# A two-layer GRU run in chunks: 32 steps and 16 times 62 in place of 16 times 64

## The chip, the cores and the metric

The kernel runs on one NeuronCore of a Trainium2 chip. The metric is the device time of one execution in microseconds (us). Engines are named as the profile names them: PE is the matrix engine (PEld its weight load), DVE the vector engine, ACT the scalar engine, POOL the GpSimd engine, SP the engine that issues most DMAs. "L324" is line 324 of the kernel before.

## What is computed

The input is x, two sequences (b) of 1024 tokens of 256 numbers, and a context vector for each sequence. A residual block with a two-layer GRU comes first, then a residual mixture of experts over all 2048 tokens. Cut to what matters here:

```
mixed = tanh(x @ W_in.T + b_in + context)
for layer in (0, 1):                        # h starts at zero for each sequence
    xr, xz, xn = split(x_t @ Wih.T + bih)   # x_t: mixed, or layer 0's h
    hr, hz, hn = split(h @ Whh.T + bhh)
    r, z = sigmoid(xr + hr), sigmoid(xz + hz)
    n = tanh(xn + r * hn)
    h = (1 - z) * n + z * h                 # 1024 steps, each needs the one before
x = x + (gate * h2 + h2) @ W_out.T + b_out  # gate: of the context
x = x + (shared(x) + two best of 8 experts(x)) / 3
```

All arithmetic that matters is in float32.

## The kernel before, in words

**Chunks.** The 1024 steps of a sequence are cut into J = 16 chunks of S = 64 steps. With B = 2 sequences that makes R = 32 rows, and one step of a layer does all 32 rows at once. A chunk's true start state is the end of the chunk before it, which is not known yet. So layer 0 goes through its chunks twice: a first pass of `AHEAD[0]` = 64 steps from zero, whose end states, moved on by one row, are the start states of the second pass, which gives the outputs. The row of each sequence that holds its first chunk starts the second pass from zero. Layer 1 starts its first pass 44 steps ahead (`AHEAD[1]`) and runs `LAG` = 2 ticks behind layer 0. After the second pass `fit` (L441) compares the end state of each row with the start state that the next row was given. If any of the 128 partitions is off by more than 2^-18 of the largest start value (`TOL`), a branch at L678 does all 1024 steps one after the other and repeats the rest.

**Layout.** Tokens are kept in the order (step in chunk, b, chunk), 32 columns to a step: a *group*. `x_sb` holds x, `hs1` layer 1's outputs, `inputs` the 64 groups of layer 0's input sums, all on chip. A state lies in two forms: units on partitions, `h` (128 x 2 x 32), for the matrix engine, and a *row* form (128 x 64, four quarters of the units times 32 rows) for the gates. One 32x32-block transpose on DVE (L332) goes from the second to the first.

**A step of a layer.** `add_state` (L262): 8 matmuls of the state with `Whh` into a PSUM bank that ACT has filled with the input sums (`prepare`, L460 to L466). `finish_scanned` (L296): ACT sigmoid (L305), DVE scan (L308), ACT tanh (L319), DVE L321, DVE scan (L324), DVE transpose (L332). Layer 1's input products are fed by `feed` (L468).

**Ticks.** The loop at L594 is written out: tick t does layer 0's step and, while layer 1 runs, layer 1's. `position` (L453) tells the step in the pass: 0 is the first of the second pass. In the kernel before, layer 0 is alone in ticks 0 to 21, both layers run in ticks 22 to 127, and layer 1 is alone in 128 and 129: 130 ticks, 128 + 108 = 236 layer steps.

**Work placed between the steps.** The input side is made in pieces while the loop runs: 16 *mix* pieces (L207: 4 matmuls and two tanh for half of 8 groups) and 64 *input* pieces (L386: 8 matmuls, and a DVE add at L396 for one group). `work_of` (L503) gives a tick of layer 0 alone three units of pieces (a mix counts two), and a tick of both layers one piece. The order is fixed by `pieces_in_turn` (L522), and the pieces must be there before the step that reads them. In the second pass `plan` (L557) places, for each 8 finished groups, the output projection (L805), the adding to x (L816), the transposing back to tokens (L821, L843), the router (L832) and the store of the tokens to DRAM (L877). The order on each engine in this loop is the order of the program text.

**Pass change.** At position 0 `begin_from` (L437) clears one column for the two first chunks and hands on the state tile moved by one column, and `turned` (L432) makes its row form. Both stand at the top of the tick. Behind the loop come the last group of 8, the fit, and the mixture of experts (`moe`, L899), which the change leaves as it is.

Of the kernel before, what the change touches and what calls it, by code (L numbers as in the profile page):

```python
# [17 lines left out]
P = 128  # L18
# [12 lines left out]
J = R // B  # L31
S = T // J


AHEAD = (64, 44)

# [23 lines left out]
EARLY = 8  # L60
FILL = EARLY + 1


# [8 lines left out]
def gru_moe(ctx, tc, xT, vec, bias, w_in, wih0, whh0, wih1, whh1, w_out, w_gate, router, w1, w3, w2, w1e, w2e, out):  # L72
# [29 lines left out]

    inputs = const.tile([P, S, 4, U], FP, name="inputs")
    room = inputs.rearrange("p s c u -> p s (c u)")
# [9 lines left out]
    for k in range(KD):  # L114
        nc.vector.tensor_scalar(
            mix_bias[:, k, :],
            vec_sb[:, COND + k * B : COND + (k + 1) * B],
            vec_sb[:, B_IN + k : B_IN + k + 1],
            None,
            ALU.add,  # L120
        )

    class Steps:
# [171 lines left out]

        def finish_scanned(self, layer, to, tick, before_n, after_n, between):  # L296

# [33 lines left out]
            )  # L331
            nc.vector.transpose(to, row[:, :, 1])  # L332
            self.rows[layer], self.states[layer] = row[:, :, 1], to

# [25 lines left out]
    with ExitStack() as stack:  # L360
# [23 lines left out]
        spread(0)  # L384

        def input_piece(i):  # L386

            ps = g.bank("ps_in")[:, 0 : 3 * U].rearrange("p (c u) -> p c u", c=3)

            def products():  # L390
                at = i * R % MB
                mixed = mixes[i * R // MB]
                return g.times_input(0, ps, lambda k: mixed[:, k, at : at + R], True)

            def rest():
                nc.vector.tensor_tensor(inputs[:, i, 1:4, :], ps, g.sum_bias[0][:, 1:4, :], ALU.add)  # L396

            return products, rest, lambda: None
# [18 lines left out]

        ahead = [edge.tile([P, KD, 1 + R], FP, name=f"ahead{layer}") for layer in range(2)]  # L420
        for t in ahead:
            nc.gpsimd.memset(t, 0.0)

        def given(layer, name, end):

            t = edge.tile([P, KD, R], FP, name=f"{name}{layer}")
            nc.gpsimd.memset(t, 0.0)
            for b in range(B):
                nc.vector.tensor_copy(t[:, :, b * J + 1 : (b + 1) * J], end[:, :, b * J : (b + 1) * J - 1])
            return t  # L430

# [4 lines left out]

        def begin_from(layer):  # L437
            nc.vector.memset(ahead[layer][:, :, J : J + 1], 0.0)
            return ahead[layer][:, :, 0:R]

        def fit(layer):  # L441

            off = edge.tile([P, KD, R], FP, name=f"off{layer}")
            nc.vector.tensor_tensor(off, given(layer, "end", g.states[layer]), g.starts[layer], ALU.subtract)
            off = turned(off.rearrange("p k r -> p (k r)"), f"off_row{layer}")
            most = edge.tile([P, 2], FP, name=f"most{layer}")
# [6 lines left out]
        def position(layer, tick):  # L453

            return tick - AHEAD[0] - LAG * layer

        def runs(layer, tick):
            return -AHEAD[layer] <= position(layer, tick) < S

        def prepare(layer, tick):  # L460

            if runs(layer, tick):
                return nc.scalar.copy(  # L463
                    by_sum(banks[layer][tick % 2])[:, 0:4, :],
                    g.sum_bias[1] if layer else inputs[:, position(0, tick) % S, :, :],
                )  # L466

        def feed(tick, halves):  # L468

            if halves and runs(1, tick):  # L470
                fed = h0[tick - LAG]
                return g.times_input(
                    1, by_sum(banks[1][tick % 2])[:, 1:4, :], lambda k: fed[:, k, :], False, True, halves
                )

        def let_wait(ins, copied):
# [17 lines left out]
        def input_pieces():  # L494
            for i in range(S):
                yield input_piece(i)
# [25 lines left out]
        def pieces_in_turn():  # L522

            for _ in range(MB // R, S, MB // R):
                for which in (mixing, making, mixing, *[making] * (MB // R - 1)):
# [31 lines left out]
        def plan(group):  # L557
            first = AHEAD[0] + LAG + (group + 1) * GS
            for i, (m, b) in enumerate((m, b) for m in range(KD) for b in range(B)):
# [11 lines left out]

        for group in range(S // GS - 1):
            plan(group)
# [15 lines left out]
        g.negate(nc.gpsimd, g.wih[1], 1)  # L589
        g.negate(nc.gpsimd, g.whh[1], 2)  # L590


        with tc.manual_schedule():
            for tick in range(AHEAD[0] + S + LAG):  # L594
                now = [layer for layer in range(2) if runs(layer, tick)]
                for layer in now:
                    if layer not in g.states:
                        g.states[layer], g.rows[layer] = zero_state, zero_row
                    elif position(layer, tick) == 0:
                        g.starts[layer] = g.states[layer] = begin_from(layer)  # L600
                        g.start_rows[layer] = g.rows[layer] = turned(g.starts[layer], f"start_row{layer}")
# [3 lines left out]
                for layer in now:  # L605
# [3 lines left out]
                    if layer == 0:  # L609
                        last = placed(tick, "product")  # L610
                        last = do(work, 0) or last
                        if not busy:
                            feed(tick + 1, [0])
                        to = h0_pool.tile([P, KD, R], FP, name="h0")
                        if position(0, tick) == -1:
                            to = ahead[0][:, :, 1:]
                        h0[tick] = to
                        g.finish_scanned(
# [4 lines left out]
                            lambda: copied.append(prepare(0, tick + 1)),  # L623
                            lambda: (do(work if 1 in now else [], 1), placed(tick, "scan0")),
                        )
                    else:
                        last = feed(tick + 1, range(KD) if busy or 0 not in now else [1])
                        if 0 not in now:
                            placed(tick, "product")
                        to = hs1[:, :, cols(position(1, tick) % S)]  # L630
                        if position(1, tick) == -1:
                            to = ahead[1][:, :, 1:]
                        g.finish_scanned(
# [4 lines left out]
                            lambda: prepare(1, tick + LAG),  # L638
                            lambda: (0 in now or placed(tick, "scan0"), placed(tick, "scan1")),
                        )  # L640
                if 1 not in now:
                    do(work, 1)
# [21 lines left out]

            front.all_of(g.bank, S // GS - 1, rest_of_hidden)
            assert not places
# [11 lines left out]
    with tc.If(n_fit < P):  # L678
        with ExitStack() as stack:

            g = Steps(stack, "_turn", on_pe=True, rest_of_x=lambda: load_x(0, N))
            all_mixed = room[:, 0 : KD * N // D, :].rearrange("p (k s) d -> p k (s d)", k=KD)
            for n0 in range(0, N, MB):
# [8 lines left out]
            for t in (*turn_rows, *turn_states, column):  # L692
                nc.vector.memset(t, 0.0)
            with tc.For_i(0, T, 1) as t:
                chunk = t >> (S.bit_length() - 1)
                chunk.max_val = J - 1
                n = (t & (S - 1)) * R + chunk
                for b in range(B):
# [8 lines left out]
                for b in range(B):  # L707
                    for k in range(KD):
                        nc.vector.tensor_copy(hs1[:, k, bass.ds(n + b * J, 1)], turn_states[1][:, k, b : b + 1])
            for group in range(S // GS):  # L710
                front.all_of(g.bank, group)
# [5 lines left out]
class Front:  # L717
# [133 lines left out]
    def hid(self, m, n):  # L851

        more = self.room[:, NT + ROWS : S, :].rearrange("p (m s) d -> p m (s d)", m=KS - KD)
        return self.h1[:, m, n] if m < KD else more[:, m - KD, n]
# [453 lines left out]
```

## Time and profile before

| what | us |
|---|---|
| median of the runs shown (three: 553.87, 554.26, 555.28) | 554.26 |
| the profiled execution, its own time | 558.67 |
| its span, from first to last instruction | 556.9 |
| first L324 of the loop (tick 0) | 12.81 |
| last L324 of the loop (tick 129) | 379.12 |
| PE busy / DVE busy / ACT busy / POOL busy | 521.6 / 393.5 / 249.6 / 76.8 |

The profiled execution is 4.4 us above the median, and its span is 1.8 us shorter than its own time. Lengths of ticks are read as the distance between starts of layer 0's L324 in one tick and in the next. The loop takes 366.3 of the 556.9 us; some 13 us of loading lie ahead of it, and the rest behind it is the mixture of experts. The granted clock of the matrix engine was 0.995 over the span.

### The profile page before, as it was taken

Reading aid. Unit: us, or ns where it says so; the run is one execution under the profiler, and the core shown is the slowest. Engines: PE = TensorE matmul, PEld = TensorE weight load, DVE = VectorE, ACT = ScalarE, POOL = GpSimd, SP = SyncE. Lnnn points to the kernel's source line nnn. Section 1 sums busy time; section 2 is a strip of 40 time slices with the busy share of each in tenths; the row PEclk is TensorE's granted clock in tenths of the full one; section 3 lists DMA queues with packets and bytes.
Section 4 is the critical chain, followed back from the end, with each engine's and each line's share of the span. In section 5 each row is a group of like instructions: output and inputs, shape, how many; then the busy total and the mean of one; then the engine's idle time right before and its main releaser. Section 6 shows DMA issues by size and latency. Waiting matters only on the chain.

```text
span 556.9 us, 18850 instructions
## 1 busy us (share of the span) xinstructions
PE 521.6 (94%) x7620; PEld 345.1 (62%) x7620; DVE 393.5 (71%) x1309; ACT 249.6 (45%) x850; POOL 76.8 (14%) x131
## 2 busy tenths in 40 slices
PE   6999999999999899999989999989998999999994
PEld 3666666666555445666656656655447888864683
DVE  3776679889888788888888888897972333322395
ACT  3433356666666555556565565652122333341000
POOL 1200000000000000000000000001054444007771
PEclk9999999999999999999999999999998999999999
DMA  8970000000000000000000000002023433213253
GB/s 282 366 237 1 2 3 4 3 2 4 3 3 3 2 2 2 2 22 2 22 23 1 22 22 4 22 1 77 1 67 104 124 124 122 68 58 105 87 166 106
DMA packets 22785, 31.62 MB, mean 57 GB/s; under 512 B 3009, under 2 KB 18241, under 8 KB 22689
## 3 DMA queue, kind: packets, MB, share of 16 engines
q1 hardware_dynamic: 19328, 21.52, 11.4%
q0 software_dynamic: 3216, 8.79, 5.5%
q8 instruction: 64, 1.05, 0.8%
q14 instruction: 33, 0.26, 0.2%
q10 hardware_dynamic: 144, 0.01, 0.0%
HBM read 21.00 MB, written 9.31 MB: 54 GB/s over the span
## 4 chain that ended last, share of the span: by engine, by line
DVE 41%; PE 35%; ACT 9%; issue 6%; POOL 4%; DMA 3%; another core or an unknown queue 1%; SPq 0%; DVEq 0%; POOLq 0%; ACTq 0%
DVE row L324 14%; DVE ps_step L308 13%; DVE h L332 8%; ACT n L319 8%; PE ps_step L265 7%; PE ps_in L237 6%; PE ps_y L1134 6%; PE ps_h L1134 5%; POOL inputs L1211 3%; PE ps_w L859 3%; PE ps_mix L214 3%; DMA x_sb<-in_xT 2%; PE ps_hT L1126 1%; PE ps_step L237 1%; PE ps_xT L1126 1%
## 5 line engine op out<-in xcount | busy, mean ns | idle before, releaser
L265 PE MATMUL ps_step<-whh_sb,h 128*32 128x192 f32 x3712 | 198.0, 331 | 6.2 <-DVE h L332 5.2
L265 PEld LDWEIGHTS ps_step<-whh_sb,h 128*32 128x32 f32 x3712 | 98.1, 109 | 73.3 <-DVE h L332 53.0
L324 DVE TENSOR_TENSOR_SCAN row<-gates,n 128x128 f32<-128x128 f32 x236 | 100.3, 425 | 33.4 <-ACT n L319 33.0
L308 DVE TENSOR_TENSOR_SCAN ps_step<-gates,ps_step 128x128 f32<-128x128 f32 x236 | 99.4, 421 | 20.4 <-ACT gates L305 20.0
L237 PE MATMUL ps_step<-wih_sb,h 128*32 128x192 f32 x1712 | 106.2, 328 | 5.1 <-ACT ps_step L463 1.5
L319 ACT ACTIVATE n<-ps_step 128x64 f32<-128x64 f32 x236 | 55.0, 233 | 114.7 <-DVE ps_step L308 114.7
L305 ACT ACTIVATE gates<-ps_step 128x128 f32<-128x128 f32 x236 | 68.4, 290 | 41.7 <-PE ps_step L265 36.0
L237 PEld LDWEIGHTS ps_step<-wih_sb,h 128*32 128x32 f32 x1712 | 58.1, 109 | 33.7 <-ACT ps_step L463 20.9
L332 DVE STREAM_TRANSPOSE h<-row 128x64 f32<-128x64 f32 x234 | 57.5, 246 | 8.0
L859 PE MATMUL ps_w<-x_sb,w_sb 128*128 128x512 f32 x128 | 56.7, 596 | 0.1
L237 PE MATMUL ps_in<-wih_sb,mixed 128*32 128x192 f32 x1024 | 51.4, 327 | 2.6 <-DVE wih_sb L172 2.6
L463 ACT COPY ps_step<-inputs 128x256 f32<-128x256 f32 x128 | 49.6, 388 | 3.6 <-DVE inputs L396 3.6
L1128 DVE COPY hT<-ps_hT 128x256 f32<-128x256 f32 x35 | 14.9, 425 | 51.0 <-PE ps_hT L1126 47.5
L926 POOL IOTA lane_i<- 128x128 int32 x1 | 0.2, 240 | 366.4 <-PE ps_fit L671 366.4
L321 DVE SCALAR_TENSOR_TENSOR n<-gates,row 128x64 f32<-128x64 f32 x232 | 48.6, 209 | 0.0
L237 PEld LDWEIGHTS ps_in<-wih_sb,mixed 128*32 128x32 f32 x1024 | 33.6, 110 | 13.8 <-issue 5.0
L463 ACT COPY ps_step<-bt 128x256 f32<-128x256 f32 x108 | 40.6, 376 | 3.4
L859 PEld LDWEIGHTS ps_w<-x_sb,w_sb 128*128 128x128 f32 x128 | 23.9, 190 | 28.0 <-issue 26.3
L1163 POOL DMA_INDIRECT inputs<-given,pick x35 | 33.4, 954 | 52.6 <-PE ps_xT L1126 26.5
L1134 PE MATMUL ps_y<-w2e_sb,hT 128*128 x140 | 37.2, 389 | 3.3 <-DVE hT L1128 3.3
L1134 PE MATMUL ps_h<-w1e_sb,xT 128*128 x140 | 36.4, 383 | 0.7 <-DVE h L873 0.7
L1211 POOL DMA_INDIRECT inputs<-back,slots x32 | 31.1, 973 | 35.5 <-DMA back<-y 26.4
(168 smaller groups left out, 451.3 us busy)
## 6 DMA issues: line engine op xcount, KB each, us to landing
back<-y SPq DMA_DIRECT2D x35, 128.0 KB
w1e_sb<-in_w1e SPq DMA_DIRECT2D x1, 2048.0 KB
w2e_sb<-in_w2e SPq DMA_DIRECT2D x1, 2048.0 KB
given<-inputs SPq DMA_DIRECT2D x8, 256.0 KB
out_dram<-o SPq DMA_DIRECT2D x16, 128.0 KB
wih_sb<-in_wih SPq DMA_DIRECT2D x2, 768.0 KB
whh_sb<-in_whh SPq DMA_DIRECT2D x2, 768.0 KB
x_sb<-in_xT SPq DMA_DIRECT2D x3, 512.0 KB
```

What stands on the lines that cost most here:

```text
L237: last = nc.tensor.matmul(out=out[cols(q), :, :], lhsT=given(k), rhs=self.wih[layer][:, k, q * 3 * U : (q + 1) * 3 * U].rearrange("p (g u) ...
L265: nc.tensor.matmul(out=by_sum(self.sums[layer])[cols(q), 0:3, :], lhsT=self.states[layer][:, k, :], rhs=self.whh[layer][:, k, q * 3 * U : ...
L305: nc.scalar.activation(gates[:, :, :, 1], sums[:, 1:3, :], AF.Sigmoid)
L308: nc.vector.tensor_tensor_scan(s, gates[:, 0, :, :].rearrange("p u i -> p (u i)"), ps[:, 0 : 6 * U : 3], 0.0, ALU.mult, ALU.add,)
L319: nc.scalar.activation(n[:, :, 0], s[:, 1 : 2 * U : 2], AF.Tanh, scale=-1.0)
L321: nc.vector.scalar_tensor_tensor(n[:, :, 1], gates[:, 1, :, 1], 1.0, h, ALU.subtract, ALU.mult)
L324: nc.vector.tensor_tensor_scan(row.rearrange("p u i -> p (u i)"), gates[:, 1, :, :].rearrange("p u i -> p (u i)"), n.rearrange("p u i -> p ...
L332: nc.vector.transpose(to, row[:, :, 1])
L463: return nc.scalar.copy(by_sum(banks[layer][tick % 2])[:, 0:4, :], g.sum_bias[1] if layer else inputs[:, position(0, tick) % S, :, :],)
L859: last = self.tc.nc.tensor.matmul(out=ps, lhsT=self.later[name][:, k, m * P : (m + 1) * P], rhs=self.x1[:, k, blk * TB : (blk + 1) * TB], ...
L1134: nc.tensor.matmul(out=ps, lhsT=of[:, k, :], rhs=weights_sb[:, bass.ds(e * KD + k, 1), :], start=(k == 0), stop=(k == KD - 1),)
L1211: nc.gpsimd.indirect_dma_start(out=yb, out_offset=None, in_=back[:, :], in_offset=bass.IndirectOffsetOnAxis(ap=slots[:, i % 2, i // 2 : i ...
```

## The change

Each sequence is now 32 steps and 16 chunks of 62 (32 + 16 * 62 = 1024). In the first pass row 0 of each sequence does 30 steps whose results are thrown away; then its state is set to zero (`kept`), and in the last 32 steps of the pass it does the first 32 tokens, as final outputs, not as a trial run. In the second pass row j (1 to 15) does chunk j - 1, starting from what row j - 1 ended the first pass with, and row 0 does the last chunk, starting from row 15's end. Row 1's start is exact, so its column is taken out of the fit. Ticks: layer 0 alone in 0 to 19, both in 20 to 123, layer 1 alone in 124 and 125: 126 ticks, 124 + 106 = 230 layer steps. Layer 1's first pass stays 44 steps.

The output still has 64 groups. The two extra ones (`EXTRA` = 2) stand in front and hold the first 32 tokens of each sequence; the passes use groups 2 to 63. Row 0 thus has other inputs in the first pass (the first 32 tokens) than in the second (the last chunk), and three things move data for it: `exchange` swaps 32 columns of x for each sequence (six copies on POOL), `last_inputs` writes row 0's input sums for the second pass from groups 0 and 1 to DRAM and back to groups 32 to 63 (three DMAs from SP), and `first_outputs` copies row 0's outputs of the first pass into groups 0 and 1 (two copies on POOL). Two POOL memsets for `ahead` and two for `end` go.

The diff, cut to its core (the branch for a failed fit, whose sequential loop becomes two loops, and renamings of 64 to `GROUPS` are left out; the lines at the end, of layer 0, stand likewise for layer 1):

```diff
-S = T // J
-AHEAD = (64, 44)
+FIRST = 32
+S = (T - FIRST) // J
+AHEAD = (S, 44)
+GROUPS = N // R
+EXTRA = FIRST // J
...
+    def exchange():
+        other = const.tile([P, KD, B, FIRST], FP, name="other")
+        for to, of in ((other, None), (None, x_sb), (x_sb, other)):
+            for e in range(EXTRA):
...
+                nc.gpsimd.tensor_copy(a, b)
...
         def finish_scanned(self, layer, to, tick, before_n, after_n, between, keep=None):
...
-            nc.vector.transpose(to, row[:, :, 1])
-            self.rows[layer], self.states[layer] = row[:, :, 1], to
+            row = row[:, :, 1]
+            if keep is not None:
+                kept = self.edge.tile([P, U], FP, name=f"kept{layer}")
+                nc.vector.tensor_scalar(kept, row, keep, None, ALU.mult)
+                row = kept
+            nc.vector.transpose(to, row)
+            self.rows[layer], self.states[layer] = row, to
...
+        not_first = g.gru_only.tile([P, 1], FP, name="not_first")
+        row_i = g.gru_only.tile([P, 1], I32, name="row_i")
+        nc.gpsimd.iota(row_i, pattern=[[0, 1]], base=0, channel_multiplier=1)
+        nc.vector.tensor_scalar(row_i, row_i, J - 1, None, ALU.bitwise_and)
+        nc.vector.tensor_copy(not_first, row_i)
+        nc.vector.tensor_scalar(not_first, not_first, 1.0, None, ALU.min)
...
-        def begin_from(layer):
-            nc.vector.memset(ahead[layer][:, :, J : J + 1], 0.0)
-            return ahead[layer][:, :, 0:R]
+        def go_round(layer):
+            to, of = by_row(begin[layer]), by_row(g.states[layer])
+            nc.vector.tensor_copy(to[:, :, :, 1:J], of[:, :, :, 0 : J - 1])
+            nc.vector.tensor_copy(to[:, :, :, 0:1], of[:, :, :, J - 1 : J])
...
         def fit(layer):
...
-            nc.vector.tensor_tensor(off, given(layer, "end", g.states[layer]), g.starts[layer], ALU.subtract)
+            nc.vector.tensor_tensor(off[:, :, :, 1:J], end[:, :, :, 0 : J - 1], begun[:, :, :, 1:J], ALU.subtract)
+            nc.vector.tensor_tensor(off[:, :, :, 0:1], end[:, :, :, J - 1 : J], begun[:, :, :, 0:1], ALU.subtract)
+            nc.vector.memset(off[:, :, :, 1:2], 0.0)
...
+        def keep_of(layer, tick):
+            return not_first[:, 0:1] if position(layer, tick) == -FIRST - 1 else None
...
-            for i in range(S):
+            for i in (*range(EXTRA, MB // R), *range(EXTRA), *range(MB // R, GROUPS)):
                 yield input_piece(i)
...
         def plan(group):
-            first = AHEAD[0] + LAG + (group + 1) * GS
+            first = AHEAD[0] + LAG + (group + 1) * GS - EXTRA
...
+        def last_inputs():
+            nc.sync.dma_start(
+                out=spare.rearrange("e p d -> p e d"), in_=inputs[:, 0:EXTRA, :, :].rearrange("p e c u -> p e (c u)")
+            )
+            for e in range(EXTRA):
+                at = GROUPS - FIRST + e * J
+                nc.sync.dma_start(
+                    out=room[0:P:J, at : at + J, :], in_=spare[e, :, :].rearrange("(r i) d -> r i d", i=J)
+                )
+        def first_outputs():
+            for e in range(EXTRA):
...
+                nc.gpsimd.tensor_copy(by_row(hs1[:, :, cols(e)]), row)
+        place(AHEAD[0] - 1, "end", exchange)
+        place(AHEAD[0], "end", last_inputs)
+        place(AHEAD[0] + LAG, "end", first_outputs)
...
-                        g.starts[layer] = g.states[layer] = begin_from(layer)
+                        g.starts[layer] = g.states[layer] = begin[layer]
                         g.start_rows[layer] = g.rows[layer] = turned(g.starts[layer], f"start_row{layer}")
...
-                        if position(0, tick) == -1:
-                            to = ahead[0][:, :, 1:]
...
+                            keep_of(0, tick),
                         )
+                        if position(0, tick) == -1:
+                            go_round(0)
```

`go_round` stands right behind the layer's own step, ahead of the other layer's; `begin_from` stood at the top of the next tick. In the changed program's order of instructions `exchange`'s first two copies stand ahead of POOL's two negations of layer 1's weights (L172), and its other four behind them.

## The prediction, made before the changed kernel ran

> **What bounds the kernel now.** I read the page's busy times first, then its chain by lines, then the timeline tick by tick.
>
> ```profile
> PE 521.6 (94%) x7620; PEld 345.1 (62%) x7620; DVE 393.5 (71%) x1309; ACT 249.6 (45%) x850; POOL 76.8 (14%) x131
> ...
> DVE 41%; PE 35%; ACT 9%; issue 6%; POOL 4%; DMA 3%; another core or an unknown queue 1%; SPq 0%; DVEq 0%; POOLq 0%; ACTq 0%
> ```
>
> PE looks full, but the ends of its matmuls are modelled. In the chain (second line) DVE leads, and PE and ACT take turns with it: no engine alone sets the end, the recurrence does. The timeline (start, length, engine, line, tiles, and in brackets the idle time before) shows one turn of it, layer 0 in a tick of both layers:
>
> ```profile
> 186.23 0.43 DVE L308 TENSOR_TENSOR_SCAN ps_step<-gates,ps_step 128x128 f32<-128x128 f32 x1
> ...
> 186.96 0.42 DVE L324 TENSOR_TENSOR_SCAN row<-gates,n 128x128 f32<-128x128 f32 x1 [0.18 <-ACT n L319]
> ...
> 187.42 0.25 DVE L332 STREAM_TRANSPOSE h<-row 128x64 f32<-128x64 f32 x1
> ...
> 187.72 0.86 PE L265 MATMUL ps_step<-whh_sb,h 128*32 128x192 f32 x16
> ...
> 188.64 0.29 ACT L305 ACTIVATE gates<-ps_step 128x128 f32<-128x128 f32 x1
> ...
> 188.97 0.43 DVE L308 TENSOR_TENSOR_SCAN ps_step<-gates,ps_step 128x128 f32<-128x128 f32 x1
> ```
>
> From L308 to the next L308 is 2.74 us, each step right behind the one before. Layer 1's four DVE instructions lie in the hole, and DVE has only two pauses of 0.18 us. So a tick of both layers costs 2.74 us, by the recurrence and nearly also by DVE. An input piece fits in (ticks 33 to 44 hold one each, and last 2.734 to 2.744; ticks 46 to 62 without one last 2.734 to 2.743). A mix piece does not fit: the scans L324 of ticks 29 to 33 start at 95.11, 97.83, 101.31, 104.03 and 107.51, so the ticks with a mix cost 3.48 where their neighbours cost 2.73, that is +0.74. With layer 0 alone, PE binds instead, because the tick is filled with pieces. From the chain in order of time (start, length):
>
> ```profile
> 28.98 1.99 PE ps_in L237 x48
> 30.98 0.81 PE ps_step L265 x16
> 31.79 1.99 PE ps_in L237 x48
> ```
>
> 1.99 + 0.81 is 2.80 us. The pass change of layer 0 is the one great stall:
>
> ```profile
> 190.23 0.25 DVE L332 STREAM_TRANSPOSE ahead<-row 128x64 f32<-128x64 f32 x1
> ...
> 191.75 0.06 DVE L438 MEMSET ahead<- 128x2 f32 x1
> 191.84 0.24 DVE L434 STREAM_TRANSPOSE start_row<-ahead 128x64 f32<-128x64 f32 x1
> 191.87 0.86 PE L265 MATMUL ps_step<-whh_sb,ahead 128*32 128x192 f32 x16 [1.36 <-DVE ahead L438]
> ```
>
> The state is there at 190.48, but the clearing memset is queued on DVE behind all of layer 1's step, so PE starts at 191.87 and not some 0.3 after L332's start. That tick, from L324 to L324, is 189.70 to 193.84, 4.14 us: 1.40 too long. Layer 1's pass change (196.58 to 199.70) costs 3.12, 0.38 too long.
>
> **The change, part by part.** All differences are in starts of layer 0's L324; "too long" is against 2.74.
>
> *Ticks that go, second pass.* Layer 0's second pass has 62 ticks for 64, and the two that go are plain ones (the seven groups that are placed in it, each with one tick of about 3.45, stay seven): 2 x 2.74 = **-5.48**.
>
> *Ticks that go, first pass.* Before, ticks 19 and 20 of layer 0 alone take 2.83 and 2.79; tick 21, which also feeds layer 1 for the first time, takes 3.14, and tick 22 with a mix 3.07. After, tick 19 is the one that feeds layer 1: 3.14 again, with 1.99 us of pieces as there. Tick 20 has an input piece in place of a mix: 2.74. So two ticks go, **-5.62**, and 0.33 more with the mix, **-0.33**.
>
> *Pieces that move.* With 20 ticks of layer 0 alone there is less room: followed through the piece order, the last four mixes now stand in ticks 23, 25, 33 and 35, all of both layers; before there were two such (30 and 32) beside that of tick 22. Two more at 0.735: **+1.47**. It could be as little as 2 x 0.33 (the mix in tick 22, whose tick lacked layer 1's state products). Input pieces run to tick 48 in place of 45, which costs nothing by the ticks above. No step comes near waiting for its piece: tick 20 makes group 39 and reads group 22.
>
> *Row 0 set to zero.* One DVE multiply of 128x64 stands between L324 and the transpose in tick 29 (layer 0) and tick 31 (layer 1), on the recurrence. The nearest row is L166, 0.19 us for the same size; with the 0.04 that a dependent instruction starts behind the one before it (L324 0.42, L332 0.46 later) it is 0.23: two, **+0.46**. Bounds: nothing (below nothing is excluded, since work is only added) and 0.34 each (L761, four times the size).
>
> *Layer 0's pass change.* The two copies of `go_round` stand right behind the transpose, ahead of layer 1's step, so PE no longer waits for layer 1. Nearest row: L429, 128x30 copies, two in 0.23 us. They and `turned` (0.25, about 0.2 of DVE time beside an overlapping neighbour) still lie on DVE, which is nearly full: 0.29 + 0.24 = 0.53 too long in place of 1.40: **-0.87**. Behind the copies wait PE's state products of layer 0 (0.3 later) and layer 1's L308. What is late next is DVE itself. Bounds: -1.1 (only the copies count) and +0.3 (the old stall stays and the copies come on top).
>
> *Layer 1's pass change.* A memset of 0.06 is replaced by the same two copies: **+0.15**, between 0 and +0.6.
>
> *Fit of layer 0.* It costs 1.37 in tick 127. Two copies and a subtraction (from 374.23 to 374.72) become two subtractions and a memset: **-0.1**, between -0.2 and +0.2. Layer 1's fit ends long before PE's L859, so its change is hidden.
>
> *Nothing, with its cover.* (1) Three small DVE instructions for `not_first` before the first scan: PE holds tick 1 (products until 14.29, while tick 0's transpose ended at 13.52); without that cover about 0.4. (2) `exchange` and `first_outputs` on POOL, idle from 18.28 to 384.72: their first readers are L816 of group 0 in tick 72, eleven ticks (30 us) behind `exchange`, and L805 of group 0 in tick 70, six ticks (16 us) behind `first_outputs`. (3) `last_inputs` on SP, idle from 27.6 to the first L877 store at 240.99: 256 KB out and back, needed by ACT for tick 92, 29 ticks (79 us) behind its issue; the loads ahead of the loop ran at 282 to 366 GB/s, and at a tenth of that 512 KB take 18 us. Queued behind it on SP are only the stores of tokens, 40 us later. (4) POOL's two copies ahead of the negations L172: they need the first x load only, which was there before the first L396 at 10.91, and L172 waited for its weights until 14.81 anyway; layer 1 needs them near 70.
>
> (5) DVE slowed by POOL's new copies. POOL's two L172 run from 14.81 to 18.28, inside the loop; DVE's L321 at 15.77 (two SBUF inputs) still takes 0.21 and L324 at 16.16 takes 0.42, as elsewhere. So I take 0. Upper bound: six copies inside the loop, each holding the recurrence for a POOL row of like size (L928, 128x128, 0.29): +1.7.
>
> The Trainium skill, "SBUF — State Buffer", section "Who interferes with whom", speaks against (5): a DVE instruction with two SBUF inputs contends with a GpSimd instruction that reads SBUF, and whichever comes second blocks until the first is through. The rows above show DVE undelayed beside L172, which reads SBUF. By the rule the sum would be up to 1.7 us worse; by the rows it is unchanged.
>
> *Sum.* -5.48 - 5.62 - 0.33 + 1.47 + 0.46 - 0.87 + 0.15 - 0.1 = **-10.3 us**. Against the profiled execution, 558.67 (span 556.9), that makes 548.4, and a span of 546.6. The runs' median is 554.26, 4.4 lower; the gain is a count of ticks, so I take it whole from there: **543.9 us**. The part behind the loop is the same work on tokens in another order, and is taken as unchanged.
>
> **The rivals.**
>
> *Part of it is given back in the loop* (546.5). The stall of layer 0's pass change stays (+1.17 against my value: 0.3 above before) and POOL's copies hold DVE (up to +1.7, most of it): about -7.8. For it: DVE has only 0.36 us of pause in a tick, so anything new there shows. Against: in the new order the copies stand ahead of layer 1's step, and L172 disturbed nothing.
>
> *Four ticks come off more cleanly* (542.5). The two further mixes cost 0.33 each (-0.81), the zeroing is hidden (-0.46), and of layer 0's pass change only the copies count (-0.23): -11.8. For it: tick 22. Against: ticks 30 and 32, which are the same situation as the new ones.
>
> *The fit fails* (slower). Layer 0 has 62 steps to forget its start, and layer 1's input has settled for two fewer. The one mechanism is the comparison: once a partition is off by more than 2^-18 = 3.8e-6 of its largest start, the branch runs 1024 steps one after the other. Two layers at 2.74 each make 5.5 us a step: about 5600 us more, plus the experts once again. Worked out in double precision from the reference's inputs, the largest ratio is 2.1e-6 with 64 steps and 2.3e-6 with 62 (layer 1: 0.5e-6 in both). That is below the bound, but by a factor of 1.7 only, and the chip's roundings and activation functions aren't in it.
>
> *It does not shorten the loop.* A tick count that didn't fall, or a wait of ACT for `last_inputs`, would give 554. The changed program's order has 230 scans like L324 for 236, so this is left with next to nothing.
>
> **How the numbers follow.** About 0.3% (1.7 us) is what a measurement of this kernel can tell from no change. Forecast 0.72, given back 0.14, cleaner 0.10, fit fails 0.02, not shortened 0.02. Likeliest: 543.9. The range takes the bounds: with every cost low about -12, with all of these high (pass changes, zeroing, POOL's hold, fit) about -6.3: 542.0 to 548.0. Faster 0.96 (the first three), same 0.02, slower 0.02.
>
> **What would show it.** 230 scans; plain ticks still 2.74; L324 of tick 62 at 188.9 (that of tick 64 was at 193.84), four ticks of 3.48 in the first pass, PE's products at the pass change no longer behind layer 1's scan, the last L324 at 368.8. It would be wrong if plain ticks changed (POOL or DMA beside them, or another clock), if ACT's copies waited for DMA near tick 92, or if the part behind the loop moved by more than 1 us.

## The result and the profile after

The changed kernel takes **545.39 us** (median of four runs, 545.05 to 545.48), the one before 554.27 (553.87 to 555.28): the ratio is 0.9836, 95% interval 0.9819 to 0.9853. That is 8.9 us less; 10.3 were forecast (543.9). Its profiled execution took 545.48 with a span of 543.8, so this one lies at its median, while that of before lies 4.4 above its own.

The page after: the line of busy times, and the chain by engine.

```profile
PE 510.7 (94%) x7492; PEld 340.5 (63%) x7492; DVE 387.6 (71%) x1292; ACT 244.5 (45%) x832; POOL 82.7 (15%) x136
...
DVE 40%; PE 34%; ACT 10%; POOL 7%; issue 5%; DMA 3%; SPq 0%; POOLq 0%; DVEq 0%; ACTq 0%
```

PE and DVE do less, POOL does 5.9 us more, and POOL's share of the chain that ended last went from 4 to 7%. Of POOL's 5.9 us the eight new copies are only 2.5 (two of them run ahead of the loop); most of the rest lies behind the loop, in work that the change does not touch.

Lines move: the scan L324 is now L347, L308 is L331, the transpose L332 is L360, `add_state`'s products L265 are L287. Layer 0's pass change in the timeline (start, length, engine, line, tiles, in brackets the idle time before):

```profile
186.30 0.25 DVE L360 STREAM_TRANSPOSE h<-row 128x64 f32<-128x64 f32 x1
186.58 0.19 DVE L470 COPY begin<-h 128x60 f32<-128x60 f32 x1
186.69 0.16 DVE L471 COPY begin<-h 128x4 f32<-128x4 f32 x1
...
186.91 0.86 PE L287 MATMUL ps_step<-whh_sb,begin 128*32 128x192 f32 x16 [0.25 <-DVE begin L471]
...
188.11 0.20 DVE L462 STREAM_TRANSPOSE start_row<-begin 128x64 f32<-128x64 f32 x1
...
188.93 0.42 DVE L347 TENSOR_TENSOR_SCAN row<-gates,n 128x128 f32<-128x128 f32 x1 [0.19 <-ACT n L342]
```

The two copies stand right behind the transpose, and PE starts 0.61 us behind the transpose's start, where it was 1.64 before. The tick is 3.08 us long (4.15 before), and tick 62's scan starts at 188.93 (forecast 188.9). The last scan starts at 368.67 (forecast 368.8). Row 0 set to zero, in tick 29:

```profile
96.27 0.42 DVE L347 TENSOR_TENSOR_SCAN row<-gates,n 128x128 f32<-128x128 f32 x1
96.73 0.25 DVE L358 TENSOR_SCALAR kept<-row,not_first 128x64 f32<-128x64 f32 x1
97.01 0.24 DVE L360 STREAM_TRANSPOSE h<-kept 128x64 f32<-128x64 f32 x1
```

**Where the time went.** From tick 1's scan to the last one took 362.96 us before and 352.81 after: **-10.15**, and in repeated executions of both kernels 362.98 and 352.98. So the loop gave what was forecast, to 0.15. Behind the loop, everything up to the experts' first activation is the same to 0.01 us. From ACT's last copy of the experts' rows (L1179 before, L1261 after; below, before and then after) the program took 59.92 us to the end of its span before and **61.40** after. That is where the rest went.

```profile
496.95 0.37 ACT L1179 COPY y<-ps_y 128x256 f32<-128x256 f32 x1 [1.49 <-PE ps_y L1134]
```

```profile
482.35 0.37 ACT L1261 COPY y<-ps_y 128x256 f32<-128x256 f32 x1 [1.49 <-PE ps_y L1216]
```

Between those two parts the profiled execution of before has a pause of about 4 us in the experts that the one of after has not; it is taken up at the end and is no part of the 8.9.

### The profile page after: what moved, and what is told of

Same layout as the page of the kernel before. It is cut to its first block, busy times and chain, and to the rows that moved or that the text cites. A ratio compares the mean times of both kernels' runs of the same rounds, so it can differ in the third digit from the quotient of the medians.

```text
span 543.8 us, 18557 instructions
## 1 busy us (share of the span) xinstructions
PE 510.7 (94%) x7492; PEld 340.5 (63%) x7492; DVE 387.6 (71%) x1292; ACT 244.5 (45%) x832; POOL 82.7 (15%) x136
## 4 chain that ended last, share of the span: by engine, by line
DVE 40%; PE 34%; ACT 10%; POOL 7%; issue 5%; DMA 3%; SPq 0%; POOLq 0%; DVEq 0%; ACTq 0%
DVE row L347 15%; DVE ps_step L331 13%; DVE h L360 8%; ACT n L342 8%; PE ps_step L287 6%; PE ps_y L1216 6%; PE ps_h L1216 6%; POOL inputs L1293 6%; PE ps_in L259 5%; PE ps_w L941 3%; PE ps_mix L236 3%; DMA x_sb<-in_xT 2%; PE ps_hT L1208 1%; PE ps_xT L1208 1%; PE ps_x L887 1%
## 5 line engine op out<-in xcount | busy, mean ns | idle before, releaser
L287 PE MATMUL ps_step<-whh_sb,h 128*32 128x192 f32 x3616 | 192.9, 331 | 6.5 <-DVE h L360 5.4
L287 PEld LDWEIGHTS ps_step<-whh_sb,h 128*32 128x32 f32 x3616 | 95.7, 109 | 71.7 <-DVE h L360 51.5
L347 DVE TENSOR_TENSOR_SCAN row<-gates,n 128x128 f32<-128x128 f32 x230 | 97.6, 425 | 31.6 <-ACT n L342 30.9
L331 DVE TENSOR_TENSOR_SCAN ps_step<-gates,ps_step 128x128 f32<-128x128 f32 x230 | 96.8, 421 | 19.2 <-ACT gates L328 19.0
L259 PE MATMUL ps_step<-wih_sb,h 128*32 128x192 f32 x1696 | 103.0, 328 | 4.5 <-ACT ps_step L504 1.7
L342 ACT ACTIVATE n<-ps_step 128x64 f32<-128x64 f32 x230 | 53.5, 233 | 112.6 <-DVE ps_step L331 112.6
L328 ACT ACTIVATE gates<-ps_step 128x128 f32<-128x128 f32 x230 | 66.7, 290 | 38.9 <-PE ps_step L287 33.1
L360 DVE STREAM_TRANSPOSE h<-row 128x64 f32<-128x64 f32 x228 | 56.0, 246 | 8.0
L504 ACT COPY ps_step<-inputs 128x256 f32<-128x256 f32 x124 | 48.1, 388 | 2.3 <-DVE inputs L426 2.3
L344 DVE SCALAR_TENSOR_TENSOR n<-gates,row 128x64 f32<-128x64 f32 x224 | 46.9, 209 | 0.0
L504 ACT COPY ps_step<-bt 128x256 f32<-128x256 f32 x106 | 39.9, 377 | 3.3
L1293 POOL DMA_INDIRECT inputs<-back,slots x32 | 32.7, 1021 | 35.2 <-DMA back<-y 26.7
L1216 PEld LDWEIGHTS ps_y<-w2e_sb,hT 128*128 128x128 f32 x140 | 26.4, 190 | 5.1 <-DVE hT L1210 1.5
```

The source lines that it names most:

```text
L259: last = nc.tensor.matmul(out=out[cols(q), :, :], lhsT=given(k), rhs=self.wih[layer][:, k, q * 3 * U : (q + 1) * 3 * U].rearrange("p (g u) ...
L287: nc.tensor.matmul(out=by_sum(self.sums[layer])[cols(q), 0:3, :], lhsT=self.states[layer][:, k, :], rhs=self.whh[layer][:, k, q * 3 * U : ...
L328: nc.scalar.activation(gates[:, :, :, 1], sums[:, 1:3, :], AF.Sigmoid)
L331: nc.vector.tensor_tensor_scan(s, gates[:, 0, :, :].rearrange("p u i -> p (u i)"), ps[:, 0 : 6 * U : 3], 0.0, ALU.mult, ALU.add,)
L342: nc.scalar.activation(n[:, :, 0], s[:, 1 : 2 * U : 2], AF.Tanh, scale=-1.0)
L344: nc.vector.scalar_tensor_tensor(n[:, :, 1], gates[:, 1, :, 1], 1.0, h, ALU.subtract, ALU.mult)
```

## The experiments

The forecast's theory: the loop is worth a count of ticks, the moves cost nothing, and the part behind the loop is unchanged. Rivals: the moves cost time; part of the gain is the new pass change and not the ticks; and, once the result was there, that the missing 1.4 us lie in how the gathers behind the experts fall against the work beside them.

**The two kernels again.** before_again and after_again are the kernels unchanged.

> The kernel before, unchanged, profiled once more. Theory A: the first profile of the kernel before held a pause of about 4 us among the experts that most executions do not have (its own time was 558.67, the median 554.3). So this profile has a span near 552.5, its last L324 again near 379.1, the first expert's L1174 again near 413.3, and the gathers L1211 a rhythm of 1.43 us nearly throughout. Theory B: the pause belongs to the kernel, and the gain was had among the experts too: then the span is near 557 again.

> The changed kernel, unchanged, profiled once more. Theory A: 545.4 again (ratio to before 0.984), the last scan L347 near 368.7, and a run of the last 14 gathers L1293 at 1.73 us each, where the kernel before has 1.43: that costs 14 times 0.3, less what the better part before it saves, and is what is missing of the 10.3 us. Theory B: the slow rhythm is chance of one execution; then this profile has 1.43 and the time is still 545.4.

Measured: 1.0001 (0.9980 to 1.0023) times before, and 0.9827 (0.9798 to 0.9856). On that chip both kernels were some 6 us slower (560.4 and 551.2), and both profiles have the pause in the experts that is told of at the end. So the span of 552.5 that the first theory gave for before_again missed (556.1), and of after_again's first theory the ratio and the last scan came (369.1), but not the 14 gathers at 1.73: there the turn is 1.44 us nearly throughout, as it is 1.43 in before_again. The slow rhythm is thus not in every execution of the changed kernel. The loop came out alike to 0.2 us, which is why the experiments are read by the loop's own length, and the rest by its own.

**The moves left out.** `exchange`, `last_inputs` and `first_outputs` are not called; groups 0 and 1 are filled with zeros.

```diff
-        place(AHEAD[0] - 1, "end", exchange)
-        place(AHEAD[0], "end", last_inputs)
-        place(AHEAD[0] + LAG, "end", first_outputs)
```

> The changed kernel without the three moves of row 0's data: no exchange, no last_inputs, no first_outputs in the loop (groups 0 and 1 of layer 1's output are zeroed instead, so the first 32 tokens and the last chunk's inputs are not the reference's). Theory A: the moves cost nothing in the loop: last scan within 0.3 us of the changed kernel's, time within 0.5 us of 545.4 unless the end falls into another rhythm. Rival: POOL's copies hold DVE, or the DMAs hold ACT: up to 1.7 us faster, with shorter ticks where the copies ran.

Measured: 352.9 for the loop, 0.9828 (0.9801 to 0.9855) in all. The eight copies on POOL and three DMAs cost nothing that can be measured.

**POOL beside the loop, at ten times the size.** The moves being free could be luck of timing, so pool_flood puts 96 copies on POOL, 26.2 us for the 2.5 of the eight. Two thirds of them follow `exchange` from 114 us on; the last 32 stand behind `first_outputs` and run from 194 us.

```diff
+        def flood():
+            for _ in range(16):
+                nc.gpsimd.tensor_copy(idle, x_sb[:, 0, 0:64])
+        for t in range(AHEAD[0] - 1, AHEAD[0] + 5):
+            place(t, "end", flood)
```

> The changed kernel with 96 further copies on GpSimd, 128x64 out of x_sb, which begin once the exchange of inputs has ended (near 114 us) and lie beside ticks 35 to 45 of both layers. This is the disputed term of the prediction at some twenty times its size. By the rows (GpSimd's negations did not delay VectorE): these ticks last 2.74 as before, and the copies alone get longer. By the rule that whichever of the two comes second waits (VectorE with two SBUF inputs, GpSimd reading SBUF): VectorE has four such instructions in a tick, each late by up to a copy of 0.25, so ticks of 3.0 to 3.7 and 3 to 10 us in all.

The rows of 114 to 130 us, in which the first of them ran (line, engine, operation, count, busy us, mean ns, idle): POOL and then DVE in pool_flood, and DVE in the changed kernel.

```profile
L661 POOL COPY idle<-x_sb 128x64 f32<-128x64 f32 x48 | 13.0, 271 | 2.9
```

```profile
L347 DVE TENSOR_TENSOR_SCAN row<-gates,n 128x128 f32<-128x128 f32 x12 | 5.2, 431 | 1.3 <-ACT n L342 1.3
...
L344 DVE SCALAR_TENSOR_TENSOR n<-gates,row 128x64 f32<-128x64 f32 x11 | 2.3, 209 | 0.0
```

```profile
L347 DVE TENSOR_TENSOR_SCAN row<-gates,n 128x128 f32<-128x128 f32 x12 | 5.1, 425 | 1.3 <-ACT n L342 1.3
...
L344 DVE SCALAR_TENSOR_TENSOR n<-gates,row 128x64 f32<-128x64 f32 x11 | 2.3, 211 | 0.0
```

POOL is busy for 13 of 16 us, and DVE's instructions with two SBUF inputs are as long as without it (431 for 425 ns, 209 for 211); two scans, which began with 0.2 us of a copy still to run, took 0.48 and 0.51. The copies vary instead: most take 0.24, some 0.36 to 0.45. 23 copies began within a scan L347, and 22 of them, however early or late, ended 0.03 us behind the scan's end (the other began in its last 0.02): they were held until the scan was through. The loop took 353.05. So the cost of nothing was right and the upper bound of 1.7 us was far too careful. The Trainium skill's page "SBUF — State Buffer", section "Who interferes with whom", has the one that comes second wait; here the contention shows, but what waits is POOL, nearly always.

**The pass change, apart from the ticks.** late_round calls `go_round` at the top of the next tick, where the kernel before had its memset; before_early does the reverse to the kernel before.

```diff
-            nc.vector.memset(ahead[layer][:, :, J : J + 1], 0.0)
...
+                        if position(0, tick) == -1:
+                            nc.vector.memset(ahead[0][:, :, J : J + 1], 0.0)
```

> The changed kernel with go_round moved to the top of the next tick, behind the other layer's step, where the kernel before has its memset. Theory A: layer 0's pass change is again bound by DVE's order: its tick (L347 to L347) is 4.2 to 4.5 us in place of 3.08, layer 1's 3.3 as it is: 1.1 to 1.4 us later at the last scan, 546.5 to 546.9 in all. Rival: the place of the copies is of no account because something else starts the tick; then 545.4.

> The kernel before, with the one memset of each pass change moved right behind the layer's own step, ahead of the other layer's. Theory (the stall at layer 0's pass change is the memset's place in DVE's queue, not the change itself): the scan after it comes 2.8 to 3.1 us behind the one ahead of it, for 4.15 before, layer 1's stays at 3.1; from tick 1's scan to the last scan about 361.8 for 363.0; the time about 1.1 us below the kernel before, which is inside the scatter. Rival (the stall belongs to having a pass change at all): 4.1 stays and nothing moves. If the theory holds, some 1 us of the change's 10 in the loop has nothing to do with fewer ticks.

In late_round the copies come behind layer 1's transpose, and PE waits 1.42 us:

```profile
187.87 0.24 DVE L360 STREAM_TRANSPOSE h<-row 128x64 f32<-128x64 f32 x1
188.04 0.15 DVE L470 COPY begin<-h 128x60 f32<-128x60 f32 x1
...
188.32 0.86 PE L287 MATMUL ps_step<-whh_sb,begin 128*32 128x192 f32 x16 [1.42 <-DVE begin L471]
```

The tick is 4.21 long in place of 3.08, the loop 353.99 (0.9829, 0.9800 to 0.9857, in all, on the noisier chip). In before_early the tick falls from 4.15 to 2.99, the loop to 361.45, and the time to 552.78, 0.9979 (0.9968 to 0.9990) of the kernel before. So the stall was the memset's place in DVE's queue, and 1.1 (the tick) to 1.5 (the loop, which takes 362.6 to 363.0 in the three other executions of this loop) of the change's 10 us are to be had without it.

**Half of the change.** first16 has `FIRST = 16`: 16 steps and 16 times 63, 128 ticks.

> The changed kernel with 16 steps for row 0 ahead of 16 times 63, so 128 ticks, all the moves being there. Theory (a tick that goes is worth 2.74 us in the second pass and 2.8 in the first, and the moves cost next to nothing): from tick 1's scan to the last one 358.0 for 352.9 after and 363.0 before (two ticks more than after, +5.5, and the mix of tick 21 cheaper by 0.4); four ticks with a mix, 21, 23, 31 and 33, the first of them about 3.1 to 3.5; the time some 5 us above the changed kernel. Rival (part of the gain comes from the new pass change and the early round alone): from tick 1's scan to the last one 361 or more, since then half of the ticks brings less than half of the gain.

Measured: 358.04 for the loop (forecast 358.0); 550.67 us, 0.9944 (0.9931 to 0.9956). Its end is as late as that of the changed kernel (61.2 us behind the experts' last row), so the total shows less than the loop.

**The mixes halved.** split_mix does 128 columns at a time, eight halves where there were four pieces in ticks of both layers.

```diff
-                            rhs=x_sb[:, k, n0 : n0 + MB],
+                            rhs=x_sb[:, k, n0 + c0 : n0 + c0 + HB],
```

> The changed kernel with each mix piece halved (128 columns in place of 256), one half in a tick. Theory (a mix costs 0.735 us in a tick of both layers because its 256 columns hold PE too long beside two state products, and half of it fits as an input piece does): the four ticks of 3.47 go, all ticks of both layers in the first pass cost 2.74 to 2.8, from tick 1's scan to the last one about 350 for 352.9. Rival (the cost is a fixed one of each piece, by its eviction or its place in the queue): eight halves at 0.4 to 0.7 each, 353 to 356. The time follows by the same amount.

Neither came: 352.32 for the loop. The eight ticks with a half take 2.98 to 3.00, so a half costs 0.25 where a whole one costs 0.73: it nearly fits. PE in one of them:

```profile
82.72 0.84 PE L289 MATMUL ps_step<-whh_sb,h 128*32 128x192 f32 x16
83.50 0.71 PE L238 MATMUL ps_mix<-x_sb,w_in_sb 128*128 128x128 f32 x4
84.14 0.86 PE L289 MATMUL ps_step<-whh_sb,h 128*32 128x192 f32 x16
```

The half takes 0.71 us where a whole one took 1.13 (ticks 4 and 5 of the changed kernel): it runs from 83.50 to 84.21, up against layer 0's next products at 84.14. Of the 0.90 that this saves, 0.52 is given back in tick 2, where the new order of pieces makes the tick 3.32. The total is 545.05, 0.9834 (0.9821 to 0.9846).

**The gathers behind the experts.** POOL brings the experts' rows back by 32 gathers (L1293 after), and between them does a one-element copy (L1292) that makes it wait for work on the other engines. POOL's rows behind the loop, in before_early (there the code is that of the kernel before, and its execution has no pause in the experts) and after:

```profile
L1214 POOL DMA_INDIRECT inputs<-back,slots x32 | 32.0, 999 | 35.0 <-DMA back<-y 26.4 <-POOL inputs L1213 5.7 <-issue 2.9
L1213 POOL COPY inputs<-o 1x1 f32<-1x1 f32 x11 | 3.6, 326 | 0.1
```

```profile
L1293 POOL DMA_INDIRECT inputs<-back,slots x32 | 32.7, 1021 | 35.2 <-DMA back<-y 26.7 <-POOL inputs L1292 5.7 <-issue 2.9
L1292 POOL COPY inputs<-o 1x1 f32<-1x1 f32 x11 | 3.8, 342 | 0.1
```

The timeline of POOL in before_early, and later in after, there with the DVE sum beside the copy, shows the turn:

```profile
513.22 0.18 POOL L1213 COPY inputs<-sig 1x1 f32<-1x1 f32 x1
513.66 0.97 POOL L1214 DMA_INDIRECT inputs<-back,slots  x1 [0.27 <-POOL inputs L1213]
514.64 0.18 POOL L1213 COPY inputs<-silu 1x1 f32<-1x1 f32 x1
```

```profile
514.89 1.06 POOL L1293 DMA_INDIRECT inputs<-back,slots  x1 [0.27 <-POOL inputs L1292]
...
515.82 0.48 DVE L1321 SCALAR_TENSOR_TENSOR inputs<-inputs,share 128x256 f32<-128x256 f32 x1
515.96 0.38 POOL L1292 COPY inputs<-o 1x1 f32<-1x1 f32 x1
...
516.62 1.11 POOL L1293 DMA_INDIRECT inputs<-back,slots  x1 [0.27 <-POOL inputs L1292]
```

Left to itself the turn is 0.97 + 0.18 + 0.28 = 1.43 us. Beside DVE's sums (L1321, two SBUF inputs, 0.48 each) the copy takes 0.33 to 0.39 and the gather's issue 1.06 to 1.12, which makes the turn 1.73, just the time that PE takes for a tile in the same stretch (DVE's L1318 waits for PE and starts every 1.73 us). That is no chance: the copy starts 0.01 us behind the gather's issue, but within a sum, and all 14 such copies of after end 0.04 us behind the end of their sum, late starters and early ones alike. So POOL is held until the sum is through, as in pool_flood, and takes over DVE's rhythm, which is PE's; apart from single turns, once it falls into step it stays there to the end and never makes up for a late start. Why the gather's issue is longer too is open. In before_early the last 7 turns are in step, in after the last 13; POOL's last gather starts 48.08 and 49.81 us behind the experts' last row, a difference of 1.73, one tile. Then the last sum waits 0.39 us for it. In the five executions with the pause POOL does not fall into step for good: most turns are 1.43 to 1.44 to the end, and from the experts' last row to the end it takes 59.83 to 60.92 us, whichever the kernel. no_pace takes the copies away, in the changed kernel; before_no_pace, in the one before.

```diff
-        if behind is not None:
-            nc.gpsimd.tensor_copy(yb[0:1, 0:1], behind[0:1, 0:1])
```

> The changed kernel without GpSimd's small copies between the gathers that bring the experts' rows back. They are there for order only, so the output is unchanged. Theory (the gathers back are bound by GpSimd's own turn of 1.43 us, of which the copy is 0.18 plus its wait for VectorE): the turn falls to 1.1 to 1.25 where the buffers are free, and the program ends 1 to 4 us sooner. Rival (the buffers or the sums on VectorE bind, the copy only waits in their place): the turn stays 1.43 and nothing moves. The loop is the same as in the changed kernel.

> The kernel before without GpSimd's small copies between the gathers that bring the experts' rows back. Theory (what the change lost against its 10 us in the loop, it lost in these gathers, where it comes to run in step with VectorE four turns sooner and ends one PE tile later): here the end moves by 1.0 to 1.3 us only, to some 553.2, where the changed kernel gained 2.4 by the same edit (545.4 to 543.0); so without pacing the change is worth 10.2 and not 8.9. Rival (the loss lies elsewhere, and the copies cost both kernels the same): about 551.9, and the change is worth 8.9 here as well. The profile tells too: from the last expert's row product to the end 58.8 by either, but 1.0 to 1.1 less than the kernel before by the first.

no_pace, POOL's timeline:

```profile
515.78 0.95 POOL L1291 DMA_INDIRECT inputs<-back,slots  x1 [0.30 <-issue]
517.03 0.95 POOL L1291 DMA_INDIRECT inputs<-back,slots  x1 [0.30 <-DVE o L1319]
518.29 1.12 POOL L1291 DMA_INDIRECT inputs<-back,slots  x1 [0.30 <-DVE inputs L1319]
```

The turn falls to 1.25, with a few of 1.35 to 1.48. From the experts' last row to the end it is now 58.83 us in **both** kernels, for 61.40 and 59.83. The times are 543.00 (0.9800, 0.9788 to 0.9813) and 552.98 (0.9973, 0.9962 to 0.9983). So the copies cost the changed kernel 2.4 us and the one before 1.4, and without them the change is worth 552.98 - 543.00 = 10.0 us, all of it the loop's (9.92 between these two executions, 10.15 between the first two).

**How near the branch was.** tight_fit halves the bound of the comparison (`TOL = 2.0**-19`).

> The changed kernel with the comparison's bound halved, from 2^-18 (3.8e-6) to 2^-19 (1.9e-6). The ratio worked out in double precision is 2.3e-6. If the chip's own ratio is as worked out, the branch is taken: 1024 steps of both layers at 2.74 each, about 5600 us more, some 6150 in all. If the chip's ratio is below 1.9e-6 the time stays at 545. It tells how near the fall-back was, and what it costs.

The branch was taken, so the chip's ratio lies between 1.9e-6 and 3.8e-6, as the 2.3e-6 worked out. But it took **14721 us**, 14175 more and not 5600. From its page:

```profile
L274 PE MATMUL ps_step<-part,picks 128*32 128x256 bf16 x8192 | 1298.3, 618 | 5353.8 <-PEq L783 5185.5
...
L768 DVE COPY column<-inputs 128x1 f32 x4096 | 629.7, 154 | 2850.4 <-PEq L783 1626.5
L777 DVE COPY h<-turn_state 128x1 f32 x4096 | 629.3, 154 | 1403.4 <-DVE h L777 785.5
```

A step of the branch takes 13.4 us (from one first copy L777, at 1999.94, to the next, at 2013.32). Eight DVE copies of single columns stand in each, about 0.55 apart, with a bias product and a turn of the loop (PE idle for it 5185 us in all), and a layer's step has seven DVE instructions where the loop has four.

**Further along the same road.** first48 has `FIRST = 48`, `AHEAD = (S, 48)` and no pacing copies: 48 steps and 16 times 61, 124 ticks.

> The changed kernel without the pacing copies, and with 48 steps ahead of 16 times 61, layer 1 starting 48 steps ahead in place of 44: 124 ticks. Theory (ticks count, and a mix in a tick of both layers costs 0.73): two ticks less (-5.5), six mixes in ticks of both layers in place of four (+1.5), one zeroing less (-0.2): the loop from tick 1's scan to the last one 348.5 for 352.7, the time about 538.8 for 543.0. Rival (the fit: worked out in double precision the largest ratio is 3.5e-6 with 61 steps, a tenth below the bound): the branch is taken and the time is above 6000.

Measured: **539.97 us**, 0.9740 (0.9726 to 0.9753) of the kernel before and 3.0 below no_pace: the fastest of all. The loop is 349.59 and not 348.5: layer 1 now begins in tick 15, beside small products of the context, ahead of which PE stands idle for 0.69 us, and that tick takes 4.01. No run took the two apart. The fit held, though the ratio worked out, 3.5e-6, is only a tenth below the bound: it is a margin on these inputs, and by tight_fit the price of losing it is 14 ms.

## Why the prediction was right, and where it failed

All lengths are from one tick's scan to the next; "measured" compares the two profiled executions.

| step of the sum | forecast | measured |
|---|---|---|
| second pass, two plain ticks (2.73 to 2.745) | -5.48 | -5.48 |
| first pass: ticks 19 to 22 become 19 and 20 | -5.95 | -5.84 |
| two more mixes in ticks of both layers | +1.47 | +1.42 |
| row 0 set to zero, twice | +0.46 | +0.49 |
| layer 0's pass change, 4.15 to 3.08 | -0.87 | -1.07 |
| layer 1's pass change, 3.12 to 3.33 | +0.15 | +0.21 |
| fit | -0.1 | +0.01 |
| tick 4, 3.13 in place of 2.79 | 0 | +0.34 |
| before's tick 94 (2.97) has no like | 0 | -0.23 |
| **loop** | **-10.3** | **-10.15** |
| part behind the loop (the pause not counted) | 0 | about +1.5 |

The two sums make -8.65; the 0.2 to the medians' -8.9 is less than what the start scatters (tick 1's scan starts at 15.1 to 16.5 us, in executions of either kernel).

- **The ticks** were right, and independently: first16 came out at the 358.0 that the same prices give. That the whole loop came to within 0.15 is partly luck: single terms missed by up to 0.34, both ways (tick 19 too, 3.25 and not 3.14), and cancel.
- **Pieces that move**: ticks 23, 25, 33 and 35 take 3.44 to 3.47, as said. "Cleaner" falls with that and with the zeroing, though its third part, that of the pass change only the copies count, came true.
- **Layer 0's pass change** went 0.2 further than the sum: PE starts 0.31 us later than in a plain tick (0.61 and not 0.30 behind the transpose's start), which is nearly all of the 0.34 by which the tick is too long, so `turned` costs next to nothing. Of "given back" nothing is left, since its stall (late_round) and POOL's hold (pool_flood) both did not come.
- **Tick 4** was not foreseen. There the scan waits for ACT's filling of the next bank, L504, in place of L342:

```profile
27.39 0.43 DVE L347 TENSOR_TENSOR_SCAN row<-gates,n 128x128 f32<-128x128 f32 x1 [0.52 <-ACT ps_step L504]
```

It does so in every changed kernel, no_moves too, and not in the kernel before. The cause stays open.
- **POOL's copies** cost nothing that can be measured, as said, but not because the two engines don't disturb each other: by pool_flood they do, and POOL waits.
- **The failed step** is "The part behind the loop is the same work on tokens in another order, and is taken as unchanged." By the prediction's own sign, a move of more than 1 us, it was wrong there. The work was the same; its phase was not. That is shown by no_pace and before_no_pace, which end alike. Why POOL falls into step six turns sooner was not shown. The first gather back starts 3.06 us behind the experts' last row in after and 2.80 in before_early. But from 3.06 to 4.61 (first16 4.01, split_mix 4.61) the last one starts at the same 49.81, as it would if a late start counts in whole tiles.
- **The 4.4 us** between the profiled execution and the median of before were rightly left out. Nearly all of it is a pause in the experts: from their first activation to their last it took 79.02 us in that execution, and 74.88 in after and in the seven later profiles, of either kind of kernel, that have no such pause.
- **The rival with the fit** had its mechanism and place right and its price wrong by 2.5 times: it priced the branch at the loop's own 2.74 a step, which no row supported.

## What to carry to other kernels

In a recurrence that is written out tick by tick, a change is worth the ticks that it takes away, each at the length of a like tick in the trace, and this was good to 0.2 us in 10, with misses of up to 0.34 in single terms that cancelled. "The same work" behind it is not the same time: where an engine is held by a neighbour and falls into its rhythm, it loses whole turns (here 1.73 us at the end, with starts 0.26 us apart), and not in every execution, so look for an instruction that ends just behind the neighbour's turn after turn, and take it away if it can be spared. And price a fall-back from the instructions of its own loop, not from the fast path.

## What the runs showed of the hardware

In five of thirteen profiled executions (tight_fit not counted), of both kernels and in all four on the chip of before_again, PE, ACT and DVE stand still together for 2 to 5 us at the start of the experts, with a releaser that the profile cannot name. In the kernel before, first the timeline, then the stretches (us, busy time of each engine, PEclk, DMA share, GB/s):

```profile
420.83 0.42 DVE L1128 COPY hT<-ps_hT 128x256 f32<-128x256 f32 x1 [3.50 <-remote]
```

```profile
417.00:421.00 4.00, 2.04 (x12) 1.46 (x10) 0.50 (x2) 0.46 (x2) 3.08 (x4) 1.00 0.38 116
421.00:425.00 4.00, 3.69 (x12) 3.08 (x13) 1.53 (x4) 0.76 (x2) 1.51 (x3) 0.57 0.23 52
```

PE was idle for 2.27 us, and then its clock was granted at 0.57 for four. In the other four executions the idle time was 2.38 to 3.81 us, and two of them show the low clock (0.51 over 7 us, 0.61 over 4) and two do not. An idle time of 3.80 us lowered it and one of 3.79 did not. The Trainium skill's page "TensorE: Matmul & The Clock Gate", section "Part 1: The HAM clock gate (the "warmup" mystery)", has a window of about 3.4 us that runs freely decide, and with such a window the same gap may or may not halve the clock. That 2.27 us were enough does not follow from it, since it asks for an idle window. What the pause itself waits for is open.
